# A fourth stage of edges in a four-layer graph network on one core

## The chip, the cores and the metric

The kernel runs on one NeuronCore of one Trainium2 chip. The metric is the device time of one execution, in microseconds (us). The kernel before took 7771.67 us, the median of 10 runs (7760.12 to 7788.72).

## What is computed

A graph has 12,500 nodes with 32 features and 400,000 edges, sorted by their destination. Four layers follow each other; each adds its result to the node features and normalises them. Cut to what matters here:

```python
edge_index = jnp.stack([src, dst])
x = _layernorm(x + _L0_gnn_ref(x, src, dst, ...))       # attention
x = _layernorm(x + _L1_gnn_ref(x, edge_index, 3))       # 3 rounds of means
x = _layernorm(x + _L2_gnn_ref(x, edge_index, edge_attr_32, W1, b1, W2, b2))
x = _layernorm(x + _L3_gnn_ref(x, edge_index))          # 3 rounds of weighted sums

# L2, the edge layer
h = relu(concatenate([x[rol], x[col], edge_attr]) @ W1 + b1)
v = h @ W2 + b2
x_cand = segment_max(v, col)                            # maximum over a node's edges
return maximum(x_cand, x)

# L3, one of its three rounds
x = segment_sum(norm[:, None] * x[src], dst)
```

The destinations are drawn as 12500 u², so low node numbers have many edges and the last ones few.

## The kernel before, in words

**Blocks and counts.** The nodes lie in 98 blocks of 128. A matrix of counts `A` (how many edges lead from node to node) is built in DRAM in layer 0, as 25 chunks of 512 destinations, each with all 98 source blocks. A round of layers 1 and 3 is then a dense product: for each chunk, each of its four quarters of 128 destinations, and each source block, one matmul with the counts as weights and `x3` (the node values as three bfloat16 parts side by side, 96 columns) as moving data (L369). A few pairs that don't fit in `A` go through an extra matrix `Ax`: one row of 392 matmuls ahead of the chunks (L364) and 16 small ones in each chunk (L271). `post3` then scales a chunk and makes the next round's `x3` from it, on VectorE and ScalarE (`split`, L253 to L257).

**The edge layer.** The 308 columns of 128 edges that lead to the first block are handled apart (`heavy`). The other 2817 columns are cut into stages. A stage is a range of edges, laid out as 128 runs side by side, one on each partition. `cuts` (L212 to L217) gives each stage's end: enough columns that all edges to the nodes below block `HS[s]` lie inside it, with five standard deviations to spare. With `HS = (52, 78)` the cuts are 308, 2292, 2804 and 3125: stages of 1984, 512 and 321 columns. Inside `edge_layer`, the plan cuts a stage into batches of up to 48 columns, and a batch into groups of four. For each group POOL gathers four source rows (`ef`, L110, called in `fetch`), TensorE transposes them (L1705), and two matmul layers follow (L1736 to L1760). A batch's destination rows are filled in by 32 scans (`spread`, L1582), its maxima taken by 32 scans (`maxima`, L1591).

**What sets the order.** Python generators are advanced by hand, once for each group: `fill(0)` and `fill(1)` (work of other layers), `steps(6)` (the queue of scans) and `tick()` (ends of stages). When the last maxima of a stage are through, `end(s)` joins the ticked ones. It carries maxima over the borders between the 128 runs: three transposes, a gather `fx`, a maximum, a scatter, spread over 13 ticks, so that nothing has to wait for a transfer. `done(s)` follows: it gathers the maximum at each node's last edge (`ends`, one gather for each node block), and finishes the nodes of blocks `hs[s]` to `hs[s+1]`: norm, scale, `split` into `x3`. Then these blocks can already take part in round 0 of layer 3, and `round_part(s)` joins the fillers: for each of the 25 chunks, `x3` of each block as weights and the counts of that block (128 x 512) as moving data (L1320), then eight small matmuls that add up and turn the result (L283), a copy on ScalarE (L1327) and an addition into `part` on VectorE (L1305). Its counts come in tiles `a` with room for `HP` blocks, three in rotation (L1314, L1315); a chunk's blocks are divided evenly over as few tiles as fit.

```python
            size = -(-(hi - lo) // -(-(hi - lo) // HP))
```

`fill` advances the fillers by 16 matmuls for each group (40 once at the start of a part). After the last group the queues are drained in this order:

```python
    steps(10 ** 6)
    while later:
        tick()
```

and, behind `edge_layer`, `while fillers: fill(0)`. The last stage has no early part. Its blocks are done in round 0 proper:

```python
            R.product(x3, post3, (), 0 if r else HS[-1])
```

Round 0 multiplies only source blocks from `HS[-1]` on (its `lo`), loads only their counts (L351), and `post3` adds `part`. Its row L364 over `Ax` still needs all 98 blocks.

The instructions come into each engine's queue in an order that a scheduler draws up at compile time: program order is the priority, and an instruction whose inputs come late in the scheduler's reckoning lets later ones go ahead. Tiles of a closed pool give their memory to the next one, whose first writer then waits for the last reader.

Of the kernel before, what the change touches and what calls it, by code (L numbers as in the profile page):

```python
# [57 lines left out]

SPAN = 60.0
ONE = 512.0  # L60
HS = (52, 78)
EARLY = 2
HC = 308
SLOTS = 512
# [3 lines left out]
@with_exitstack  # L68
def gnn_resnorm_kernel(
    ctx: ExitStack,  # L70
    tc: tile.TileContext,
    x: bass.AP,
    src: bass.AP,
    dst: bass.AP,
    edge_attr: bass.AP,
    w1T: bass.AP,
    w1_b: bass.AP,
    w2: bass.AP,
    w2T: bass.AP,
    w2_b: bass.AP,  # L80
    aT: bass.AP,
    m_W1: bass.AP,
    m_b1: bass.AP,
    m_W2: bass.AP,
    m_b2: bass.AP,
    out: bass.AP,
):
    nc = tc.nc
    E = src.shape[0]
    flags = ctx.enter_context(tc.tile_pool(name="flags", bufs=1))  # L90
    bad_i = flags.tile([P, 1], I32, name="bad_i")
    dense_path(tc, bad_i, x, src, dst, edge_attr, w1T, w1_b, w2, w2T, w2_b, aT,
               m_W1, m_b1, m_W2, m_b2, out)
    general = nc.values_load(bad_i[0:1, 0:1], min_val=0, max_val=E)
    with tc.If(general > 0):
        general_path(tc, x, src, dst, edge_attr, w1T, w1_b, w2, w2T, w2_b, aT,
                     m_W1, m_b1, m_W2, m_b2, out)
# [22 lines left out]
def dense_path(ctx, tc, bad_i, x, src, dst, edge_attr, w1T, w1_b, w2, w2T, w2_b, aT,  # L120
# [90 lines left out]

    hs = (0,) + HS + (H,)  # L212
    cuts = [HC]
    for h in HS:
        f = (h * P / N) ** 0.5
        cuts.append(-(-int(E * f + 5 * (E * f * (1 - f)) ** 0.5) // P // 4) * 4)
    cuts.append(C)  # L217
    heads = []
    for s in range(len(HS) + 1):
        heads.append((  # L220
# [245 lines left out]
    def edge_tables():  # L466

        with tc.tile_pool(name="e_prep", bufs=2) as prep:
            CP = -(-C // 12)
            d0 = prep.tile([P, 1], F32, name="d0", bufs=1)  # L470
            run = prep.tile([P, 1], F32, name="run", bufs=1)
            for s in range(len(HS) + 1):
                e0, Cs = P * cuts[s], cuts[s + 1] - cuts[s]
# [169 lines left out]
    with ExitStack() as build:  # L643
# [164 lines left out]
        def slots():  # L808
# [31 lines left out]
            yield  # L840
            for s, h in enumerate(HS):
                w = slice(h % 4 * (P // W), h % 4 * (P // W) + 1)
# [310 lines left out]
    with ExitStack() as st:  # L1153
# [3 lines left out]
        with tc.tile_pool(name="seg", bufs=1) as seg, \  # L1157
# [18 lines left out]
            nc.vector.tensor_scalar(tot, tot, -1.0, 0.0, op0=OP.add, op1=OP.max)  # L1176
            for s in range(len(HS) + 1):
                sl = slice(hs[s], hs[s + 1])
# [67 lines left out]
    with ExitStack() as st:  # L1246
# [1 line left out]
        ap = st.enter_context(tc.tile_pool(name="l3_a", bufs=3))  # L1248
        psum = st.enter_context(tc.tile_pool(name="psum", bufs=1, space=PSUM))
        G = 8  # L1250
        HP = 16
        fillers = []
        first = []

# [38 lines left out]
        def round_part(s):  # L1293

            lo, hi = hs[s:s + 2]
            size = -(-(hi - lo) // -(-(hi - lo) // HP))
            late = []
# [11 lines left out]
            for c in range(NQ):  # L1309
                nq = min(4, H - c * 4)  # L1310
                y = psum.tile([P, CH], F32, name="y", bufs=2)
                for h0 in range(lo, hi, size):
                    n = min(size, hi - h0)
                    a = ap.tile([P, 4, HP, Q], F8, name="a")  # L1314
                    nc.sync.dma_start(  # L1315
# [1107 lines left out]
```

## Time and profile before

| | us |
|---|---|
| median of 10 runs | 7771.67 |
| the profiled execution | 7785.55 |
| its span | 7783.8 |
| first and last start of an edge gather `ef` | 2940.3, 6601.1 |
| PE / DVE / ACT / POOL busy, whole span | 6703.9 / 3932.2 / 1633.7 / 3531.5 |
| mean granted clock of TensorE | 0.835 |

How to read it: the span is one execution on the chip; 1.75 us of the profiled execution's time lie around it. PE is TensorE, PEld its weight loads, DVE VectorE, ACT ScalarE, POOL GpSimd, SP the engine that issues most transfers; L1320 is line 1320 of the kernel. In a list of groups, a row has the line, engine, operation, what it writes and reads, and the count, then the busy time, the mean duration of one in ns, and the idle time ahead with what ended it. In an order of time, a row starts with start and duration. PE's matmuls overlap, so a run of n matmuls is the better measure of one than its own duration. The granted clock is a share of TensorE's full clock.

### The profile page before, as it was taken

The numbers are of one execution on the slowest core, as the hardware profiler recorded it, in microseconds if no ns is written. First come the engines' busy times: TensorE is split into PE (matmuls) and PEld (weight loads), VectorE is DVE, ScalarE is ACT, GpSimd is POOL, SyncE is SP. The second block draws the span as 40 slices with busy tenths as digits, with TensorE's granted clock in tenths as the row PEclk, the third lists the DMA queues.
The fourth block names the chain that finished last, engine by engine and source line by source line (L and its number), as shares of the span: only waits on it lengthen the run. The fifth ranks groups of instructions, "written<-read, shape, count | busy, mean of one in ns | idle before, by whom it ended". The sixth has DMA issues, their size and how long they took to land. (4 is left out here: it accounts for less than half of the span.)

```text
span 7783.8 us, 196882 instructions
## 1 busy us (share of the span) xinstructions
PE 6703.9 (86%) x85600; PEld 5342.1 (69%) x85600; DVE 3932.2 (51%) x11040; ACT 1633.7 (21%) x3386; POOL 3531.5 (45%) x3445
## 2 busy tenths in 40 slices
PE   6788999898999997888888888778669979799998
PEld 4678999888999994545555555333336636799998
DVE  6999899795443224555555555433343343411121
ACT  1234787100000002222222222211112212100000
POOL 1013400000555517777777777777777776100000
PEclk7889999999999996777777777555569969999999
DMA  1138444889999992222222222211127726699998
GB/s 50 64 126 324 187 200 196 305 322 338 336 352 352 366 340 84 55 62 55 59 55 63 55 54 59 56 54 54 48 73 242 245 72 203 218 351 361 346 358 300
DMA packets 575179, 1447.57 MB, mean 186 GB/s; under 512 B 108407, under 2 KB 269791, under 8 KB 560863
## 3 DMA queue, kind: packets, MB, share of 16 engines
q1 hardware_dynamic: 433200, 1347.10, 47.3%
q0 software_dynamic: 110240, 66.25, 4.3%
q10 hardware_dynamic: 30864, 21.54, 0.9%
q8 instruction: 673, 11.03, 0.6%
q14 instruction: 202, 1.65, 0.1%
HBM read 1155.33 MB, written 279.27 MB: 184 GB/s over the span
## 5 line engine op out<-in xcount | busy, mean ns | idle before, releaser
L110 POOL DMA_INDIRECT ef<-table,ids x2817 | 2675.7, 950 | 883.0 <-issue 646.4
L369 PE MATMUL y<-x,a 128*128 128x96 bf16 x49980 | 2261.6, 207 | 115.7 <-issue 79.4
L369 PEld LDWEIGHTS <-a 128*128 128x128 fp8e4 x49980 | 2177.8, 98 | 147.5 <-issue 106.4
L1705 PE MATMUL pT<-ident,ef 128*96 128x128 f32 x2817 | 768.4, 355 | 583.2 <-DMA ef<-table,ids 564.8
L1705 PEld LDWEIGHTS pT<-ident,ef 128*96 128x96 f32 x2817 | 397.0, 161 | 1040.1 <-DMA ef<-table,ids 702.1
L1707 DVE COPY eT<-pT 96x512 f32<-96x512 f32 x705 | 476.7, 676 | 1047.8 <-PE pT L1705 1047.5
L983 PE MATMUL pa<-oh,ol 128*128 128x196 bf16 x4928 | 725.9, 271 | 120.0 <-DVE oh L973 77.2
L1754 PEld LDWEIGHTS pv<-mw,hT 128*128 128x128 f32 x3208 | 598.0, 260 | 267.3 <-issue 93.9
L989 ACT ACTIVATE at<-pa 128x784 uint16<-128x784 f32 x816 | 646.9, 824 | 508.2 <-PE pa L983 480.9
L277 DVE TENSOR_REDUCE v<-y 128x128 f32<-128x384 f32 (+2 forms) x152 | 83.3, 548 | 1270.5 <-PE y L271 1270.0
L1754 PE MATMUL pv<-mw,hT 128*128 128x64 f32 x3208 | 679.4, 349 | 21.0 <-ACT hT L1741 13.8
L1741 ACT ACTIVATE hT<-ph,mb 128x256 f32<-128x256 f32 x802 | 379.8, 474 | 1326.6 <-PE ph L1738 1301.9
L1019 PE MATMUL y<-x,at 128*128 128x102 bf16 x9604 | 646.1, 210 | 9.9 <-DVE x L257 5.4
L983 PEld LDWEIGHTS <-ol 128*128 128x128 bf16 x4928 | 552.6, 149 | 132.7 <-issue 75.7
L1736 PE MATMUL ph<-eT,mw 96*64 96x256 f32 x1410 | 628.1, 539 | 12.0 <-DVE eT L1707 10.6
L1738 PE MATMUL ph<-eT,mw 96*64 96x256 f32 x1408 | 630.3, 541 | 0.0
L973 DVE TENSOR_TENSOR oh<-bins_h,pl 128x1568 bf16<-128x1568 bf16 x616 | 594.4, 965 | 0.0
L110 POOL DMA_INDIRECT g<-code_d,ws_i x25 | 219.6, 8785 | 790.8 <-DVE ki L760 527.8
L1019 PEld LDWEIGHTS <-at 128*128 128x128 fp8e4 x9604 | 560.3, 98 | 23.2 <-issue 10.6
L115 POOL DMA_INDIRECT sorted_d<-hrow,pos x308 | 368.7, 1197 | 372.5 <-issue 203.5
L1320 PE MATMUL y<-a,x 128*96 128x512 fp8e4 (+1 forms) x1950 | 493.6, 390 | 1.6 <-DVE x L257 1.5
L968 DVE TENSOR_TENSOR ol<-la,lb 128x1024 bf16<-128x1024 bf16 x616 | 419.4, 683 | 73.2 <-PE pa L983 72.6
(406 smaller groups left out, 7000.4 us busy)
## 6 DMA issues: line engine op xcount, KB each, us to landing
a<-A SPq DMA_DIRECT2D x245, 3136.0 KB
A<-at SPq DMA_DIRECT2D x98, 1568.0 KB
a<-A SPq DMA_DIRECT2D x144, 832.0 KB
ef<-table,ids POOLq DMA_INDIRECT x2817
starts_d<-rows SPq DMA_DIRECT2D x44, 1024.0 KB
attr<-in_edge_attr SPq DMA_DIRECT2D x57, 768.0 KB
begin<-starts_d SPq DMA_DIRECT2D x57, 768.0 KB
scan<-o SPq DMA_DIRECT2D x57, 768.0 KB
```

The source lines that it names most:

```text
L110: return nc.gpsimd.indirect_dma_start(out=o, out_offset=None, in_=tab, in_offset=IndirectOffsetOnAxis(ap=idx, axis=0))
L369: nc.tensor.matmul(y[:, q, :], block(h, q - q0), x3[:, h, :3 * F], start=(q + h == first), stop=False)
L973: nc.vector.tensor_tensor(oh, bins_h[:, None].to_broadcast([P, 4, HJ, 2]), pairs(pl[:, t, 0, half * 64 + w0:half * 64 + w0 + 8])[:, :, Non ...
L983: nc.tensor.matmul(pa[:, 2 * b + i, :HJ], ols[t][:, :, :, 4 * u + 2 * b + i].rearrange("p a b -> p (a b)"), ohs[t][:, 2 * u + b, :, i], st ...
L989: nc.scalar.activation(at[:, qd, :, off:off + 8].rearrange("p h (w j) -> p h w j", w=4), pa[:, :, :HJ].rearrange("p w (h j) -> p h w j", h ...
L1019: nc.tensor.matmul(y[0][:, q, :], at[:, q - 2 * half, h, :], x3[:, h, :3 * F0], start=(q + h == 0), stop=(c < EARLY and last and q == 2 * ...
L1320: nc.tensor.matmul(y[:3 * D, :nq * Q], x3[:, h, :3 * D], a[:, :nq, h - h0, :], start=(h == lo), stop=(h == hi - 1))
L1705: nc.tensor.transpose(pT[:3 * D, j, :], B.ef[:, t + j, :], ident)
L1707: behind = nc.vector.tensor_copy(eT[:, :k], pT[:3 * D, :k])
L1736: nc.tensor.matmul(ph[:HID, :ka], mw1, eT[:, :ka], start=True, stop=True)
L1738: nc.tensor.matmul(ph[HID:2 * HID, :k - 2], mw1, eT[:, 2:k], start=True, stop=True)
L1754: nc.tensor.matmul(pv[:, j].rearrange("p h d -> p (h d)"), hT[:, j, :], mw2, start=True, stop=True)
```

## The change

Two constants change. The edge layer's stages now end behind node blocks 52, 78 and 90, and at the last block, 98; so there are four `end`s and `done`s, three early parts (52, 26 and 12 blocks), and round 0 proper starts at block 90. The tiles of counts for the early parts have room for 13 blocks instead of 16.

```diff
-HS = (52, 78)
+HS = (52, 78, 90)
...
-        HP = 16
+        HP = 13
```

With it `cuts`, `hs` and `heads` get one entry more, and with each entry come four small tiles in `heads`, one more tile `lastd`, gathered ahead of the first edge, and one more pass of the loops over stages in `edge_tables`, `slots` and the computation of `end_i`.

## The prediction

> **What bounds the kernel now.** I read the page first (where the early parts and the gathers stand), then busy time by windows, then PE's, DVE's and POOL's order around the end of the edge layer, then the chain that ended last. On the page two groups matter:
>
> ```profile
> L110 POOL DMA_INDIRECT ef<-table,ids x2817 | 2675.7, 950 | 883.0 <-issue 646.4
> ...
> L1320 PE MATMUL y<-a,x 128*96 128x512 fp8e4 (+1 forms) x1950 | 493.6, 390 | 1.6 <-DVE x L257 1.5
> ```
>
> One gather holds POOL 0.95 us plus 0.30 us of issue, so 1.25 us a column. L1320 is the early part of round 0: 78 node blocks by 25 chunks, 1950 matmuls. Windows of the edge layer's end:
>
> ```profile
> 6300.00:6400.00 100.00, 59.57 (x189) 27.96 (x189) 38.09 (x139) 13.17 (x35) 75.76 (x79) 0.57 0.20 54
> ...
> 6500.00:6600.00 100.00, 100.00 (x593) 63.59 (x592) 36.04 (x143) 20.83 (x49) 67.66 (x73) 1.00 0.67 211
> ```
>
> Columns: length, then busy PE, PEld, DVE, ACT, POOL, granted clock, DMA share, GB/s. Where no early part runs, POOL bounds (79 gathers in 100 us). Where the part of stage 1 runs, PE is busy 100 of 100 us at full clock, and POOL gets only 73 gathers through. So PE bounds the last 150 us of the edge layer already. Then PE's own order:
>
> ```profile
> 6629.82 7.09 PE L1320 MATMUL y<-a,x 128*96 128x512 fp8e4 x32
> ...
> 6642.69 2.25 PE L1320 MATMUL y<-a,x 128*96 128x256 fp8e4 x19
> 6645.45 0.63 PE L283 MATMUL z<-S,ys 96*128 96x32 f32 x4 [0.51 <-ACT ys L1327]
> 6656.38 5.87 PE L364 MATMUL y<-a,x 128*96 128x128 fp8e4 x78 [10.29 <-issue]
> ...
> 6682.35 18.81 PE L364 MATMUL y<-a,x 128*96 128x128 fp8e4 x298 [1.40 <-DVE x L257]
> ```
>
> The part of stage 1 isn't hidden to its end: the last edge gather starts at 6601.1, and the part ends at 6645. Then PE is almost idle until 6682, while 20 `ends` gathers (6646 to 6671) and the norm of the last 20 blocks run. The row L364 follows, and the 20-block product until 6825.
>
> **The change, part by part.** *The plan.* The cuts become 308, 2292, 2804, 3008, 3125. Stages 0 and 1 stay. The old last stage of 321 columns (seven batches, 81 groups of four) becomes 204 (44, 44, 44, 44, 28) and 117 (40, 40, 37), again 51 + 30 = 81 groups, in eight batches. Early part loads stay at 13 blocks in stages 0 and 1, since 52 and 26 divide into 13s with HP at 16 or 13: the smaller buffer costs nothing there.
>
> *When the new part can start.* Each group is one turn of `steps(6)` and of `tick()`. The third stage's last batch has 7 turns, 42 steps, against 64 queued (32 maxima of the batch before, 32 scans of the next): 22 are left. The next ten turns take these 22, 32 more scans and 6 of the 32 last maxima; the other 26 need a further half batch. So the maxima end 16 turns after the stage's last gathers. `end` then takes 14 turns to its first `ends` gather. 16 + 14 = 30 is all the turns that the last stage has. The same count for stage 1 gives 28 turns, and the trace shows 6157.5 (last gather) to 6295.2 (first `ends`), 137.7 us, 27.5 turns of 5.0. So the part of blocks 78 to 89 joins the fillers only in the drain, behind the stage-1 part that already overruns. All of it lies in the open behind 6645. Its blocks are ready in time: 12 gathers behind 6601 take 15 us, the norm some 10.
>
> *What it costs.* 32 matmuls of 512 columns in 7.09 us are 0.216 each; eight adders (L283) push the next by 0.81. A chunk of 12 blocks: 12 x 0.216 + 0.81 = 3.40. 24 chunks and a half one (12 x 0.118 + 0.5) make **83.6 us** of PE.
>
> *The row L364 behind it.* Its load waits for the early part:
>
> ```profile
> SPq L351 <- PE y L1320: 4.4, 1, 4.4
> ```
>
> It is issued at 6645.08, and the first matmul starts 11.3 us later. Today this lies under the wait for the last blocks; that cover goes. Its buffer can start when the early buffer under it is read out; with 25 loads more in a ring of three, that would be about two chunks before the end (3.4 + 1.9 = 5.3). Bounds 0 and 11.3; I take 6.0. The row itself is 392 matmuls:
>
> ```profile
> 6816.48 12.23 DMA a<-Ax
> ...
> 6828.85 24.18 PE y L364 x392
> ```
>
> 24.2 us after a pause of PE (21.9 for the same 392 in round 2, without one). I take 24.2.
>
> *The late product.* For 20 blocks a quarter takes PE 0.85 + 0.17 (L271); for 8 it takes 8 x 0.0425 + 0.17 = 0.51, so 2.04 a chunk instead of 4.08. DVE is next:
>
> ```profile
> 6708.87 0.56 DVE L277 TENSOR_REDUCE v<-y 128x128 f32<-128x384 f32 x1 [3.48 <-PE y L271]
> ...
> 6711.36 0.29 DVE L255 TENSOR_TENSOR rest<-v,x 128x128 f32<-128x128 f32 x1 [0.42 <-ACT x L253]
> 6712.02 0.29 DVE L257 TENSOR_TENSOR x<-rest,x 128x128 bf16<-128x128 f32 x1 [0.36 <-ACT x L256]
> ```
>
> One chunk's chain is 6708.87 to 6712.31, 3.44 us, of which 0.78 are waits for ACT. If the next chunk's operations fill these, the period is 2.66; if not, 3.44. I take 2.85, nearer the lower, because the norms of the last blocks (6668 to 6678) are interleaved in just this way. 24 chunks: 68.4 us (63.8 to 82.6). Ahead of the first reduce: 4.4 (L364's end 6701.0 to yx 6705.4) + 4 x 0.17 = 5.1. Behind the last: 3.4. Loads shrink from 640 to 256 KB. The present ones moved 276 GB/s, so 49 of 256 KB need some 47 us, below DVE's 68.
>
> The Trainium skill, "DMA: Bandwidth & Descriptors", section "Measured (HBM→SBUF, 128 partitions, SWDGE, issued from GpSimd)", speaks against shorter loads: 0.95 us for 64 KB, 6.15 for 1 MB; an estimate between them is 2.0 us for 256 KB, so 98 us for 49 one behind the other, 30 more than my term. The rows decide, since several loads are in flight here (0.87 of 16 engines busy); no run shows 256 KB yet.
>
> *Small parts.* One more `lastd` gather ahead of the edges, 1.25 us where POOL bounds. One more fx gather and scatter in the stretch that PE bounds: nothing, as a group takes 5.45 us there where POOL needs 5.0 (without that slack, 2.5). ACT's and DVE's copies for the new part queue with the norm of the last 8 blocks; DVE stood 3.41 us behind such a gather at 6664.7, so 3.4 once (0 to 7). Twelve `ends` gathers leave the drain (15 us), and the last x is ready near 6670 instead of 6682; nothing, because PE is then in the new part.
>
> *The sum*, from 6645.0 to round 1's first L364. Now 6828.85 - 6645.0 = 183.9, which includes 4.2 of waiting for its Ax load behind the last x (6824.6); that load comes early with the DMA queues emptier. New: 83.6 + 6.0 + 24.2 + 5.1 + 68.4 + 3.4 = 190.7. With 1.25 and 3.4: **+11.5 us**. The profiled execution (7785.55 us, span 7783.8 and 1.75 around it) would become 7797.0. It lay 13.9 above the median of the runs; on the median 7771.67 the forecast is **7783.2**.
>
> **The rivals.**
> *PE's clock falls in the late product (slower).* With 2.04 of every 2.85 us busy (72%), PE may lose its full clock. At half clock a chunk is 4.1 us and PE bounds: 24 x (4.1 - 2.85) = +30, so +41.5, 7813. It decides once the granted clock there is under 2.04 / 2.85 = 0.72. For it: from 6300 to 6400 PE was 60% busy at 0.57. Against it: those are f32 matmuls, and the present product holds 1.00 while 87% busy.
>
> [...]
>
> *The next round's Ax row fills PE's pauses.* Up to 24 x 0.8 = 19 us stand idle in the late product; if round 1's 392 matmuls go there, up to 16 us come back: about -5, 7767. Against it: `a` has three buffers and y three, and the row wants two of the first while chunks still turn them over.
>
> *The part is hidden after all.* Were the early part done by 6645, the last x at 6670 would start 24.2 + 5.1 + 68.4 + 3.4 = 101.1, so 6771 instead of 6829: -58, 7714. Against it: the count of turns, and PE's 100% between 6500 and 6645, where 83.6 more don't fit. So the stage changes the layout and hides nothing.
>
> **How the numbers follow.** Within 0.2% (15.5 us, about what a measurement of this kernel can tell from no change) lies 7756 to 7787. Forecast 0.62: its terms' ends give -5 (wait 0, row 21.9, 2.66 a chunk, no queueing) to +35 (11.3, 24.2, 3.44, 7); two thirds of it fall within 0.2%, a third above. Clock 0.20, slower. Ax row in the pauses 0.14, nearly all within 0.2%. Hidden 0.04, faster. Faster 0.06, same 0.53, slower 0.41. The range takes the forecast's ends, down to part of the Ax case and up to part of the clock's: 7762 to 7808.
>
> **What would show it.** L1320 should count 2250, its last 300 all behind the last edge gather and in a stretch of 80 to 90 us with PE near 100%. L369 should count 48804 (1176 less). L364 should follow within 0 to 11 us. The late product should show DVE's period near 2.85 us and PE's clock. Wrong if L1320's new matmuls lie among the edge gathers, if the late product takes over 90 us, or if the edge layer's last gather moves from 6601 by over 5 us.

## The result, and the profile after

The kernel after took 7824.37 us (median of 8 runs, 7814.41 to 7838.1), the kernel before 7771.01 us in the runs beside it: a ratio of 1.0067, 95% interval 1.0058 to 1.0076, so +53 us (45 to 59). The forecast was +11.5 us and 7783.2, the range 7762 to 7808. The direction was right; the size was not, and the time lies outside the range.

The profiled execution of the kernel after took 7818.75 us, its span 7816.6. That is 32.8 us more than the span before, less than the medians differ. About half of this gap lies ahead of the edge layer: the first edge gather starts at 2929.5 instead of 2940.3. Four later profiles on a chip of this speed have it at 2929.4 (ends_late), 2932.1 (cut_74), 2939.6 (all_three) and 2940.6 (ax_mid). Three of these kernels (all but cut_74) are the kernel after up to there, so those 10.8 us are scatter between executions and not a gain.

The page's two groups of the prediction:

```profile
L110 POOL DMA_INDIRECT ef<-table,ids x2817 | 2672.8, 949 | 879.4 <-issue 660.3
...
L1320 PE MATMUL y<-a,x 128*96 128x512 fp8e4 (+1 forms) x2250 | 569.7, 391 | 1.6 <-DVE x L257 1.3
```

The early parts have 2250 matmuls as counted, 300 more, and L369 has 48804. Windows of the kernel after, the third of them the shorter product of round 0:

```profile
6300.00:6400.00 100.00, 66.62 (x205) 31.78 (x205) 37.14 (x137) 13.03 (x36) 75.86 (x80) 0.57 0.18 51
6500.00:6600.00 100.00, 88.27 (x505) 55.30 (x505) 41.08 (x169) 18.31 (x48) 71.20 (x76) 0.93 0.61 184
6781.00:6857.00 76.00, 57.43 (x1168) 53.49 (x1166) 55.82 (x199) 14.63 (x50) 0.00 (x0) 0.95 0.64 180
```

From 6500 to 6600 PE is no longer busy all the time: 88 of 100 us, while POOL got 76 instructions through instead of 73. What the additional ones are, POOL's order of time says (start, duration, then the idle time ahead and its releaser):

```profile
6547.91 0.98 POOL L115 DMA_INDIRECT scan<-fx,fix  x1 [0.30 <-DVE fx L1638]
...
6552.97 0.95 POOL L110 DMA_INDIRECT ef<-table,ids  x1 [0.30 <-issue]
6554.22 0.94 POOL L110 DMA_INDIRECT ends<-scan,end_i  x1 [0.30 <-issue]
...
6561.71 0.94 POOL L110 DMA_INDIRECT ends<-scan,end_i  x1 [0.30 <-issue]
6562.96 0.94 POOL L110 DMA_INDIRECT ef<-table,ids  x1 [0.30 <-issue]
...
6574.19 1.14 POOL L110 DMA_INDIRECT ef<-table,ids  x1 [0.30 <-DVE ends L1264]
```

The 12 `ends` gathers of blocks 78 to 89 (6554 to 6573) stand among the edge gathers, 1.25 us each, and POOL has hardly more than its issue time between instructions there: POOL now sets the pace. The two edge gathers at 6552.97 and 6574.19 are the 92nd and the 97th of the last 117. The same two in the kernel before:

```profile
6566.13 0.94 POOL L110 DMA_INDIRECT ef<-table,ids  x1 [0.30 <-issue]
...
6573.33 0.94 POOL L110 DMA_INDIRECT ef<-table,ids  x1 [0.37 <-DVE ids L1683]
```

Counted from the first of the 117 (6431.16 after, 6443.76 before), the stream after is 0.56 us ahead at the 92nd gather, although `fx` and its scatter already lie in it, and 13.46 behind at the 97th. At the last it is 13.49 behind. So the whole lengthening of the stream falls where the 12 `ends` gathers stand. Then PE's order around the third part:

```profile
6643.68 2.25 PE L1320 MATMUL y<-a,x 128*96 128x256 fp8e4 x19
...
6665.48 1.88 PE L283 MATMUL z<-S,ys 96*128 96x32 f32 x8 [7.45 <-DVE part L1305]
6667.18 5.18 PE L1320 MATMUL y<-a,x 128*96 128x512 fp8e4 x12
...
6673.00 2.77 PE L1320 MATMUL y<-a,x 128*96 128x512 fp8e4 x12
...
6740.85 0.73 PE L1320 MATMUL y<-a,x 128*96 128x256 fp8e4 x5
...
6752.45 24.42 PE L364 MATMUL y<-a,x 128*96 128x128 fp8e4 x392 [9.73 <-DMA a<-Ax]
...
6863.80 23.41 PE L364 MATMUL y<-a,x 128*96 128x128 fp8e4 x392 [9.46 <-DMA a<-Ax]
```

The first line is the end of stage 1's part, as before near 6646. Behind it lies the whole third part, to 6741.6, with one stall of 7.45 us in which PE waits for VectorE; then 9.73 us of waiting for the `Ax` load, the row L364, the product, and round 1's row at 6863.8 instead of 6828.85. VectorE shows what PE waited for:

```profile
6652.04 0.29 DVE L1305 TENSOR_TENSOR part<-part,z 128x128 f32<-128x128 f32 x1 [4.71 <-PE z L283]
6663.79 0.43 DVE L1263 TENSOR_TENSOR ends<-ends,rest 128x256 f32<-128x256 f32 x1 [11.46 <-DMA ends<-scan,end_i]
...
6665.06 0.28 DVE L1305 TENSOR_TENSOR part<-part,z 128x128 f32<-128x128 f32 x1
```

It stood 11.46 us at the first operation of the last `done` (L1263, blocks 90 to 97) for its `ends` gathers, and the part's addition L1305 was queued behind. And SP's order has the two `Ax` loads, one early and one late:

```profile
6741.71 0.97 SPq L351 DMA_DIRECT2D a<-Ax  x2
...
6851.40 1.38 SPq L351 DMA_DIRECT2D a<-Ax  x2
```

The first is issued only when the last matmuls of the part are through (6741.58), since its tile lies on a tile of the part (ax_apart, below, shows this). The second is issued 2.9 us ahead of the product's last matmuls.

**Where the time is, in the two profiles.** The last 117 edge gathers (the new last stage) take 170.8 us from first to last start instead of 157.3: +13.5. From the last edge gather (6601.1 and 6602.0) to round 1's row L364 it is 261.8 us instead of 227.75: +34.1. Behind that it is -2.2, and between the first edge gather and the 117 columns -1.8. That is 44 us, at the lower end of the interval of the medians.

### The profile page after: what moved, and what is told of

Its sections match the earlier page's. It is cut to its first block, busy times and chain, and to the rows that moved or that the text cites. A ratio compares the mean times of both kernels' runs of the same rounds, so it can differ in the third digit from the quotient of the medians.

```text
span 7816.6 us, 195765 instructions
## 1 busy us (share of the span) xinstructions
PE 6719.1 (86%) x84924; PEld 5329.9 (68%) x84924; DVE 3940.9 (50%) x11152; ACT 1648.2 (21%) x3414; POOL 3518.7 (45%) x3449
## 4 chain that ended last, share of the span: by engine, by line
PE 49%; DMA 14%; POOL 7%; issue 5%; DVE 3%; ACT 0%; DVEq 0%; POOLq 0%; ACTq 0%; SPq 0%
PE y L369 23%; DMA ef<-table,ids 11%; POOL ef L110 6%; PE y L1320 5%; PE pv L1754 5%; PE ph L1736 4%; PE pT L1705 3%; PE ph L1738 2%; PE z L1447 1%; PE y L364 1%; DMA a<-A 1%; PE y L271 1%; PE z L283 1%; PE pT L1419 1%; POOL ends L110 1%
## 5 line engine op out<-in xcount | busy, mean ns | idle before, releaser
L369 PE MATMUL y<-x,a 128*128 128x96 bf16 x48804 | 2204.5, 207 | 119.3 <-issue 76.3
L369 PEld LDWEIGHTS <-a 128*128 128x128 fp8e4 x48804 | 2122.3, 98 | 148.9 <-issue 100.0
L1019 PE MATMUL y<-x,at 128*128 128x102 bf16 x9604 | 644.5, 209 | 10.8 <-DVE x L257 6.1
L1736 PE MATMUL ph<-eT,mw 96*64 96x256 f32 x1410 | 619.4, 532 | 11.1 <-DVE eT L1707 11.1
L1738 PE MATMUL ph<-eT,mw 96*64 96x256 f32 x1408 | 621.6, 534 | 0.0
L1019 PEld LDWEIGHTS <-at 128*128 128x128 fp8e4 x9604 | 559.1, 98 | 24.2 <-issue 11.9
L1320 PE MATMUL y<-a,x 128*96 128x512 fp8e4 (+1 forms) x2250 | 569.7, 391 | 1.6 <-DVE x L257 1.3
```

Source lines behind the costliest of these rows:

```text
L369: nc.tensor.matmul(y[:, q, :], block(h, q - q0), x3[:, h, :3 * F], start=(q + h == first), stop=False)
L1019: nc.tensor.matmul(y[0][:, q, :], at[:, q - 2 * half, h, :], x3[:, h, :3 * F0], start=(q + h == 0), stop=(c < EARLY and last and q == 2 * ...
L1320: nc.tensor.matmul(y[:3 * D, :nq * Q], x3[:, h, :3 * D], a[:, :nq, h - h0, :], start=(h == lo), stop=(h == hi - 1))
L1736: nc.tensor.matmul(ph[:HID, :ka], mw1, eT[:, :ka], start=True, stop=True)
L1738: nc.tensor.matmul(ph[HID:2 * HID, :k - 2], mw1, eT[:, 2:k], start=True, stop=True)
```

## The experiments

The theory: the loss is the third part in the open, with three waits that the prediction had priced too low: VectorE's queue in the part, the `Ax` load, and the 12 gathers in the stream. The rivals: the finer split costs time wherever the part lies; or the smaller tiles do.

The four sets ran on four chips. On three of them the kernel before takes 9061.6 to 9161.5 us, on one 7779.5; every ratio is against runs of the kernel before on the same chip. The last column is from one profile of each kernel and compares only on one chip: where the stream is the same, it still differs by up to some 11 us between the slower profiles. Only where the stages end as in the kernel after are the last 117 gathers a stage of their own.

| run | time, us | ratio to before | 95% interval | last 117 gathers, us |
|---|---|---|---|---|
| kernel before | 7771.01 | 1 | | 157.3 |
| kernel after | 7824.37 | 1.0067 | 1.0058 to 1.0076 | 170.8 |
| hp13 | 9150.62 | 0.9994 | 0.9982 to 1.0005 | 194.3 |
| split_only | 9171.74 | 1.0017 | 1.0005 to 1.0029 | 211.8 |
| fill_drain | 9218.6 | 1.0064 | 1.0040 to 1.0087 | 209.4 |
| ax_apart | 9224.45 | 1.0067 | 1.0045 to 1.0088 | 220.9 |
| after_beside | 9121.38 | 1.0072 | 1.0052 to 1.0092 | 209.1 |
| norm_later | 9118.95 | 1.0068 | 1.0049 to 1.0087 | 220.2 |
| norm_later_apart | 9114.57 | 1.0064 | 1.0046 to 1.0082 | 213.9 |
| cut_70_82 | 9077.29 | 1.0017 | 1.0005 to 1.0029 | 193.8 |
| ends_late | 7827.21 | 1.0060 | 1.0046 to 1.0073 | 171.3 |
| ax_mid | 7816.01 | 1.0051 | 1.0037 to 1.0065 | 170.2 |
| all_three | 7816.49 | 1.0046 | 1.0033 to 1.0060 | 171.9 |
| cut_74 | 7765.98 | 0.9986 | 0.9976 to 0.9996 | 151.5 |
| ends_behind | 9113.66 | 1.0043 | 1.0028 to 1.0058 | 204.9 |
| split_behind | 9067.44 | 1.0001 | 0.9988 to 1.0014 | 195.4 |
| four_edits | 9101.72 | 1.0036 | 1.0024 to 1.0048 | 195.9 |
| cut_76 | 9058.32 | 0.9989 | 0.9976 to 1.0002 | 185.5 |

### One part of the change alone

**hp13**: the kernel before with the smaller tiles.

```diff
-        HP = 16
+        HP = 13
```

> The kernel before with room for 13 blocks in the early parts' tiles instead of 16, and three stages as before. Theory (the loss is the third part in the open, the 12 gathers in the stream and the wait for Ax): no part of it is here, so 7771 within 8 us; L1320 stays at 1950, and round 1's row L364 starts near 6829. Rival (the smaller tiles, by the memory they shift, cost the time): most of +53 us, about 7810 or more.

Measured 0.9994, on a slower chip: no difference. The tiles are out as a cause of the loss.

**split_only**: the kernel after without its third part; the blocks from 78 on are done in round 0 again.

```diff
-            if s < len(HS):
+            if s < 2:
...
-            R.product(x3, post3, (), 0 if r else HS[-1])
+            R.product(x3, post3, (), 0 if r else HS[1])
```

> The kernel after with its four stages, but without the early part of blocks 78 to 89: round 0 starts at block 78 again. Theory: +12 us from the 12 ends gathers among the edge gathers, less some 10 because the last done has 8 blocks and not 20, and +1 for one lastd gather: 7771 to 7779, with L1320 at 1950 and L369 at 49980. Rival (the finer split itself, with its eighth batch, its fourth end and the order that the scheduler makes of it, costs the time, and not where the part lies): 7805 to 7824.

Measured 1.0017 (1.0005 to 1.0029), between the two: by the middle of the interval the split alone costs a quarter of the loss, and the part with its waits the rest. Its last 117 gathers took 211.8 us against 194.3 in hp13 on the same chip, +17.5. Here too the place is clear: the stream is 0.7 us behind hp13's at the 92nd of the 117 and 15.5 at the 97th, with the 12 `ends` gathers between them. So it is these gathers, and not the eighth batch or the fourth `end`, that lengthen it.

**after_beside**: the kernel after, unchanged, on one of the other chips.

> The kernel after, unchanged, on the chip of the other runs of this set, so that each of them has its own comparison. If the chip is like the first, 1.0067 times the kernel before. On a chip that grants the edge layer less clock (0.55 instead of 0.7) the tail behind the last edge gather should cost the same +34 us, since it runs at full clock there too, and the edge gathers' last 117 columns +12 to +23: a ratio of 1.005 to 1.007.

Measured 1.0072: the loss is there too.

### The stall in the part, and the wait for Ax

**fill_drain**: the part is written among the last ticks.

```diff
     while later:
         tick()
+        fill(0)
```

> The kernel after, with a fill(0) behind each tick of the drain, so that the third part is written into the program among the last done's steps and not behind them. Theory: the 7.5 us in which PE stands while VectorE waits for the last ends gather go, and most of the clock lost behind them: -8 to -12 us against the kernel after, about 7814. Rival (the wait only moves, since the norm of the last 8 blocks has then to be waited for later, or the part's additions are still queued behind it): within 3 us of 7824.

A miss: PE still stood 6.68 us for VectorE, which still stood 10.96 us at the last `done`'s first operation with the part's additions behind it. So writing the part elsewhere in the program didn't change that order; how the scheduler came to it isn't shown. The rival holds for this edit.

**ax_apart**: 2 KB a partition ahead of layer 3's tiles.

```diff
         R = Rounds(st, 1)
+        st.enter_context(tc.tile_pool(name="pad", bufs=1)).tile([P, 512], F32, name="pad")
         R.open(st)
```

> The kernel after, with 2 KB a partition left empty ahead of layer 3's tiles, so that Ax's first tile doesn't lie on the third of the early parts' tiles. Theory: the load L351 is issued at least one chunk before the early part's end, the 9.7 us in which PE waits for it shrink to 0 to 3, and the row L364 takes 22 to 24 us: -7 to -11 us against the kernel after, about 7815. Rival (the load waits for something else, or row L364 then waits for x of the last blocks): within 3 us of 7824.

The total didn't fall (1.0067), but not for the rival's reason. PE's order of this run:

```profile
8061.00 6.69 PE L1320 MATMUL y<-a,x 128*96 128x512 fp8e4 x19 [6.13 <-DMA a<-A]
8084.50 1.92 PE L283 MATMUL z<-S,ys 96*128 96x32 f32 x8 [16.81 <-ACT ys L1327]
...
8169.27 10.92 PE L364 MATMUL y<-a,x 128*96 128x128 fp8e4 x192 [0.31 <-DVE part L1305]
```

and VectorE's:

```profile
8076.72 0.43 DVE L1263 TENSOR_TENSOR ends<-ends,rest 128x256 f32<-128x256 f32 x1 [21.28 <-DMA ends<-scan,end_i]
```

The wait for `Ax` is gone (0.31 us). But the part's own first load came 6.13 us late, and this time the order had the last `done` further ahead of its gathers: VectorE stood 21.28 us, ScalarE's copies behind it, and PE 16.81. What one wait gave, two others took.

**norm_later**: the last `done` is ordered on VectorE behind the twelfth addition of the part (`adds` collects the additions of L1305).

```diff
+            if s == len(HS):
+                while fillers:
+                    fill(0)
             for t in todo:
                 yield from finish(*t)
...
+                    with tc.issue_after(adds[-14].ins):
+                        nc.vector.tensor_mul(e, e, over(rest[:, sl], k))
```

> The kernel after, with the finish of the last 8 blocks ordered behind the twelfth addition of the third part (14 from its end), so that VectorE no longer stands at the last ends gather with the part's additions queued behind it. Theory (the stall in the third part is that queueing): the part from its first L1320 to its last takes 83 to 86 us instead of 95, the wait for Ax stays near 9.7: -9 to -12 us against the kernel after. Rival (PE is held by the loads of counts or by ACT's copies in any case): the part stays at 93 or more, within 3 us of the kernel after.

From the end of stage 1's part to the end of the third it is 86.2 us, against 92.9 in after_beside on the same chip and 95.7 in the first profile: the stall was VectorE's queue, and the 83.6 us priced for the part itself were nearly right. Four of these us came back between row L364 and round 1's row (112.1 us instead of 107.9), and the medians (9118.95 and 9121.38) can't tell the two kernels apart.

**norm_later_apart**: both edits.

> The same, and 2 KB a partition left empty ahead of layer 3's tiles, so that Ax's first tile lies apart from the early parts' tiles. In the run with the empty 2 KB alone the wait for Ax went from 9.7 to 0.3 us, but VectorE stood 21.3 us at the last ends gather, and what was won was lost. Theory (two separate waits, the second hidden by nothing once the first is ordered away): -18 to -22 us against the kernel after, about 1.004 times the kernel before. Rival (a wait only moves to the next resource): no more than -10.

A miss: 6.8 us below after_beside in the medians, inside both intervals. SP's order says where it went:

```profile
7925.35 0.37 SPq L351 DMA_DIRECT2D a<-Ax  x1
...
7932.81 1.99 SPq L351 DMA_DIRECT2D a<-Ax  x1
```

The two `Ax` loads (3136 KB each) are now issued ahead of the part's loads, and PE waits for these instead:

```profile
7938.64 5.83 PE L1328 MATMUL y<-a,x 128*96 128x512 fp8e4 x19 [6.56 <-DMA a<-A]
```

The part took 99.4 us. A load of 6.3 MB that starts early is no gain where it stands in front of the loads that are needed first.

**ax_mid**: as norm_later_apart, with the `Ax` loads ordered on SP behind the part's sixteenth load.

```diff
+                    with tc.issue_after(loads[-10].ins) if lo and c < 0 else ExitStack():
                         nc.sync.dma_start(
```

> As the run with the later norm and the empty 2 KB, with the two Ax loads ordered on SP behind the sixteenth of the third part's 25 loads of counts. There they were issued ahead of the part's own loads, whose first then came 6.6 us late. Theory (the 6.3 MB of Ax are hidden only where they neither hold up the part's loads nor come behind them): the part takes 84 to 88 us and the row L364 follows within 3 us: -17 to -20 us against the kernel after, 1.0045 to 1.005 times the kernel before. Rival (DMA is full in the part, and Ax delays the loads wherever it stands): no more than -8.

1.0051 instead of 1.0067, some 12 us and not the 17 to 20 expected. Against ends_late (below), which is the kernel after in effect and ran on the same chip, it is 11 us in the medians, and the intervals overlap:

```profile
6717.94 6.95 PE L1330 MATMUL y<-a,x 128*96 128x512 fp8e4 x19 [3.96 <-DMA a<-A]
...
6752.31 22.09 PE L365 MATMUL y<-a,x 128*96 128x128 fp8e4 x392 [0.31 <-DVE part L1315]
```

The row (here line 365) follows at once and takes 22.09 us. The `Ax` loads still hold up one load of counts in the middle of the part, 3.96 us and the clock behind it, so that the part takes 94.4 us. From the end of stage 1's part to round 1's row it is 203.6 us, against 217.9 in the kernel after.

### The gathers in the stream

**ends_late**: `done` of stage 2 is written behind the last edge gather (`drained` is filled there).

```diff
             todo = []
+            while s == 2 and not drained:
+                yield
```

> The kernel after, with the done of stage 2 (blocks 78 to 89) held back until the last edge gather is written, so that its 12 ends gathers stand in the drain and not among the edge gathers. Theory (each ends gather in the stream pushes every later edge gather by its 1.25 us): the last 117 columns are 10 to 15 us shorter than in the kernel after, the third part still starts behind that of stage 1, and the total falls by the same 10 to 15: 1.005 to 1.0055 times the kernel before instead of 1.0067 to 1.0072. Rival (POOL isn't the bound there, PE is, or the gathers are only moved in front of the third part): no change against the kernel after.

No change beyond the intervals, but it tells nothing about the cost: the trace has the 12 gathers among the edge gathers all the same (6562.9 to 6581.6, the last `ef` behind them). Written later is not issued later: the order in which the program is written didn't decide where they stand.

**all_three**: ax_mid and ends_late.

> The three edits together: ends gathers in the drain, last norm behind the twelfth addition of the third part, Ax load behind its sixteenth load. Theory: -27 to -35 us against the kernel after, so still +20 to +30 against the one before (1.002 to 1.0035): what is left is the third part itself, some 84 us in the open against some 43 us from the shorter product and what the early part's end used to cover. Rival (the three waits cover each other): no better than the best of them alone.

1.0046, a miss: no better than ax_mid within the intervals. The gathers stood in the stream here too.

**ends_behind**: the gathers are tied on POOL behind the last edge gather, besides being written later.

```diff
+                    with tc.issue_after(drained[0].ins) if s == 2 else ExitStack():
+                        gather(nc, e[:, h, :], scan[:P * cuts[s + 1] - HE],
+                               end_i[:, h0 + h:h0 + h + 1])
```

> The kernel after, with the 12 ends gathers of blocks 78 to 89 tied on POOL behind the last edge gather. (Only written later, they were issued among the edge gathers all the same, so that run changed nothing.) Theory (they take POOL's time from the edge gathers where POOL bounds): the last 117 columns take 154 to 160 us as in the kernel before instead of 168, the third part still starts behind that of stage 1, -8 to -12 us against the kernel after: 1.005 to 1.0057 times the kernel before. Rival (the fourth stage slows the stream by its scans, its extra batch or PE's work): the last 117 columns stay at 166 or more and the ratio at 1.0065 or more.

Now they are moved:

```profile
7902.03 0.95 POOL L110 DMA_INDIRECT ef<-table,ids  x1 [2.77 <-DVE part L1310]
7903.29 0.95 POOL L110 DMA_INDIRECT ends<-scan,end_i  x1 [0.30 <-issue]
```

The ratio fell to 1.0043 (1.0028 to 1.0058), more than expected, but on another chip than the 1.0067 and 1.0072 that it is held against. The length that was expected (154 to 160 us) was that of the faster chip. Here the last 117 took 204.9 us, and no run on this chip has the 12 gathers in the stream to compare with.

**split_behind**: ends_behind without the third part (the edit of split_only).

> Four stages without the third early part (round 0 starts at block 78), and the 12 ends gathers of blocks 78 to 89 tied behind the last edge gather, so that the 20 ends gathers stand together as in the kernel before. Theory (what the finer split cost by itself, 1.0017, was these gathers among the edge gathers): 0.9990 to 1.0008 times the kernel before. Rival (the eighth batch, the fourth end, the schedule cost it): 1.0013 or more.

1.0001, and 1.0 lies well inside its interval, while it lay outside that of split_only. With the gathers tied behind, the eighth batch, the fourth `end` and another schedule cost nothing that is measured here. By the ratios alone this would be weak, since the two intervals overlap and the chips differ. The table's last column agrees: on the slower chips the six runs with the 12 gathers of blocks 78 to 89 in the stream took 209.1 to 220.9 us for the last 117, the six without them there 185.5 to 204.9. The firm evidence is the place of the jump, between the 92nd and the 97th gather.

**four_edits**: ax_mid with ends_behind.

> The three edits together (1.0046 times the kernel before, with the ends gathers still in the stream), now with the 12 ends gathers tied behind the last edge gather. Theory: 8 to 12 us less, 1.0030 to 1.0037: what is left is the third part in the open. Rival (the gathers in the drain hold up the third part's start or the last norm): 1.0043 or more.

1.0036, inside what was expected. The 12 gathers are out of the stream, VectorE's stall is gone and the row waits 0.32 us, and the kernel is still slower. But not every wait is gone: the `Ax` loads hold up two loads of counts (4.06 and 0.75 us), so that the part takes 96.9 us, and round 1's row still waits 8.17 us. What the part would cost without any wait was not run. An estimate from the best figures of these runs, from the end of stage 1's part to round 1's row: the part 86.2 (norm_later), the first `Ax` load 1.5 and row and lead 29.4 (ax_mid), the chunks 70.5 + 2.8 and, as before, 4.2 for round 1's `Ax` load, in all 194.6 us against 183.9. So it would still be some 11 us slower, because the part in the open costs more than the shorter product gives back.

### Other cuts

**cut_70_82**: `HS = (52, 70, 82)`.

> The kernel after with its four stages ending behind blocks 52, 70 and 82 instead of 52, 78 and 90: the stage that hides the parts is longer. By the count of turns the part of stage 1 joins the fillers some 60 turns before the last gather and that of stage 2 is done six turns before it. Theory (what counts is whether the early part lies beside the edge gathers): L1320 at 2050 with none behind the last gather's groups, round 0's product has 16 blocks, 3.4 us a chunk: 82 us instead of 76, but 95 + 9.7 us of open part go, and the old 45 us too: -80 to -110 us against the kernel after, -30 to -60 against the one before. Rival (four stages cost by themselves, or PE has no room for it among the gathers): no faster than the kernel before.

1.0017 (1.0005 to 1.0029): some 44 us faster than the kernel after on the same chip, about half of what was expected, and no faster than the one before, as the rival had it. Its tail did shrink, from the last edge gather to the end of the span 1157.1 us against 1212.8 in after_beside. The stream didn't: 4665.1 us from the first to the last edge gather, 4662.2 in after_beside. Whether the additional early blocks cost the stream on this chip, where it is slower anyway, can't be said without a profile of the kernel before there.

**cut_74**: `HS = (52, 74)`, three stages.

> Three stages, ending behind blocks 52 and 74 (and 98). By the count of turns the part of stage 1 is written 22 turns before the last gather, so that none of it is in the open; round 0's product has 24 blocks, 4.8 us a chunk on PE, 114 us instead of 98. Theory: the 45 us that the part of stage 1 stands behind the last gather today overlap the last stage's end, of which little can be saved, so the tail is 0 to 15 us shorter and the total within 0.2% of the kernel before. Rival (the overrun of the early part is all loss): -30 us or more.

0.9986, 0.9976 to 0.9996: within the 0.2% expected, and a little faster than the kernel before. No early part is in the open, yet PE has to wait for the last blocks:

```profile
6647.93 1.09 PE L364 MATMUL y<-a,x 128*96 128x128 fp8e4 x8 [22.90 <-DVE x L257]
...
6659.00 1.09 PE L364 MATMUL y<-a,x 128*96 128x128 fp8e4 x8 [9.43 <-DVE x L257]
...
6662.73 19.08 PE L364 MATMUL y<-a,x 128*96 128x128 fp8e4 x302 [1.92 <-DVE x L257]
```

So the 44 us by which stage 1's part ran over in the kernel before were largely cover for the last stage's end, as the expectation had it: from the last edge gather to round 1's row it is 223.5 us instead of 227.75.

**cut_76**: `HS = (52, 76)`.

> Three stages, ending behind blocks 52 and 76 (and 98). By the count of turns the part of stage 1 (24 blocks) is still written wholly ahead of the last gather, by 12 turns instead of 22, and round 0's product has 22 blocks instead of 24. Theory (hidden early blocks are free, late ones cost 24 x 4 x 0.0425 = 4.1 us each): 8 to 11 us less than with the cut at 74, 0.997 to 0.9975 times the kernel before. Rival (the part then reaches past the last gather again, or PE's work takes POOL's time earlier): no faster than with the cut at 74, 0.9982 to 0.999.

0.9989, 0.9976 to 1.0002, on a slower chip: the rival's figure. Two blocks more in the hidden part gave nothing that shows between different chips. Between cuts at 74 and 78 the time is flat within the intervals; by these neither cut beats the kernel before by more than 0.24%.

## Why the prediction was wrong

*Right:* the counts of matmuls; that the third part joins only in the drain and lies wholly behind the last gather; its own length (83.6 us; 86.2 without the stall); the row L364 after a pause (24.2; 24.4); nothing for the smaller tiles; and that the change hides nothing. The clock rival was nil: 0.95 from 6781 to 6857. So were the rivals that round 1's row fills PE's pauses (it starts 6.6 us behind the last `x`) and that the part is hidden.

*Right by luck:* 2.85 us a chunk of the shorter product, where 2.94 was measured. VectorE sets the pace of the first three chunks only (6783.92 to 6791.72, 2.6 us each). Behind them it waits for PE, and PE for the loads of counts (who waits for whom from 6785 to 6857: us in total, times, longest):

```profile
PE y L369 <- DMA a<-A: 15.9, 23, 1.8
DVE v L277 <- PE y L271: 14.8, 17, 2.8
```

So behind the first chunks the loads, and not VectorE, set the pace. The prediction priced them at 47 us, at the 276 GB/s of the loads of 640 KB. Those of 256 KB came at 180 GB/s while PE stood waiting for them. SP in turn waited 24.5 and 20.2 us for PE to read tiles out before it issued the next, so PE and the loads wait for each other. The last edge gather, whose move by over 5 us was to be a sign of error, stayed near 6601 (6602.0) by luck too: this execution began its gathers 10.8 us earlier, and the stream from first to last gather is 11.7 us longer.

*The step that failed first:* "Twelve `ends` gathers leave the drain (15 us) [...] nothing". They don't vanish where they leave. The prediction's count of turns put them behind the last edge gather ("12 gathers behind 6601"), 30 turns behind their stage's last gathers; the trace has the first of them at 6554.22, 23 groups of four into the last stage. There POOL pays 12 x 1.25 us for them. The prediction took PE for the bound of that stretch, with 0.45 us of slack on POOL a group, and spent that slack on `fx` and its scatter alone. For these two it was enough: the stream is 0.56 us ahead when the `ends` gathers begin. For the 12 it wasn't. POOL's waits for VectorE's `ids` between 6420 and 6620 fell from 16.3 us (19 waits) to 5.0 (6), and the stream is longer by 13.5 us, where the prediction had 1.25 (for `lastd`). hp13 and split_only show the same jump at the same place, and split_behind, without these gathers there, shows no loss.

*The terms that were mis-sized*, in the two profiles, from the end of stage 1's part on:

| term | predicted | measured |
|---|---|---|
| third part, with the queue of the last `done` | 83.6 + 3.4 | 95.65 (6645.93 to 6741.58) |
| wait for the first Ax load | 6.0 | 10.9 |
| row L364 and lead to the first reduce | 24.2 + 5.1 | 31.5 |
| 24 chunks | 68.4 | 70.5 |
| last chunk's end | 3.4 | 2.8 |
| wait for round 1's Ax load | 0 | 6.6 |
| sum | 194.1 | 217.9 |

With `lastd`, 195.35 - 183.9 = +11.5 was the forecast; with the longer stream, 217.9 - 183.9 + 13.5 = +47.5 was measured. The sum with every term at its upper end was only +35: the stream and round 1's `Ax` load were not terms of it, and the part with its stall exceeds even 83.6 + 7. The queue behind the last `done` was named, and priced by the wait of the kernel before (3.41 us). But there PE had nothing to do in it; here it stops the part, because the additions stand behind the same wait on an engine that works in order. The `Ax` wait had its upper bound at 11.3, and the measured value is next to that bound: the estimate supposed that the buffer comes free two chunks early, and the trace has the issue at the last matmul of the part. For round 1's load the prediction said that it comes early "with the DMA queues emptier". It didn't: from its issue to the first matmul of the row it is 12.4 us in both profiles. The load takes the next tiles of a ring of three, so it is issued a number of half chunks before the end, and shorter chunks make that lead shorter: 5.8 us ahead of the last `x` (6851.4 and 6857.2) where it was 8.1 (6816.5 and 6824.6).

The Trainium skill, "TensorE: Matmul & The Clock Gate", section "Why this matters for your kernels", has it that a pause of PE over some 3 us costs the clock. Behind the 7.45 us stall twelve matmuls took 5.18 us instead of 2.77, and the row L364 took 24.42 us after a wait of 9.73 and 22.09 us in ax_mid after 0.31. This agrees, and a stall of that kind costs some 2.3 to 2.4 us more than its length here.

*What stays open.* The two profiles account for 44 us (47.5 in the two stretches named) and the medians give 53 (45 to 59); single profiles scatter by as much as the rest. What the 12 gathers cost as a ratio was measured on other chips than the first. Why they were issued among the edge gathers, ahead of their turn, isn't shown.

## What to carry to other kernels

Work that is moved out of one stretch has to be priced where it goes, on each engine's queue, with that stretch's bound after the move and not before it. A wait that costs nothing today, because its engine had nothing else to do, costs its full length once useful work is queued behind it. And an early part earns only what lies beside other work: behind the last gather it is only traded, here 84 us for 42 us of a shorter product (115.7 us from the first reduce to the last `x` before, 73.3 after), and cover is lost besides. A term that comes out right can still have the wrong bound behind it: who waits for whom says whether it does.

## What the runs showed of the hardware

Chips differ far more than kernels here: 7771 to 7780 us against 9061 to 9162 for the kernel before. The difference lies ahead of round 0, mostly in the edge layer. Much the same stretch of the stream, from some 65 us behind its first gather on, in the kernel after on a chip of each kind:

```profile
3000.00:3500.00 500.00, 414.34 (x2198) 255.61 (x2198) 270.42 (x1076) 128.94 (x337) 378.10 (x401) 0.72 0.22 56
```

```profile
3300.00:3800.00 500.00, 367.75 (x1650) 226.34 (x1650) 200.16 (x783) 96.73 (x254) 283.07 (x301) 0.60 0.17 40
```

The second chip grants TensorE 0.60 instead of 0.72 and gets 301 gathers through instead of 401; the gathers themselves last the same, and POOL waits for VectorE's `ids` instead:

```profile
L110 POOL DMA_INDIRECT ef<-table,ids x2817 | 2667.9, 947 | 1926.7 <-DVE ids L1683 910.2
```

(this row is hp13's). Why the clock is lower there, and whether that belongs to these chips for good, isn't shown. From the last edge gather on, both kinds take nearly the same: 1182.7 us in the kernel before, 1189.8 in hp13.

Loads of 256 KB, of which no run of the kernel before had any in the product, moved 180 GB/s with the DMA engines busy 0.64 of the time, where the loads of 640 KB in the kernel before moved 276 GB/s at 0.88. PE waited for them 23 times, 15.9 us in all, so they held the loop up although the engines weren't full; more than three tiles in rotation were not tried. The estimate of 98 us for 49 of them one behind the other, which the prediction worked out from the Trainium skill, "DMA: Bandwidth & Descriptors", section "Measured (HBM→SBUF, 128 partitions, SWDGE, issued from GpSimd)", was too long, as several are in flight: the whole loop of chunks took 70.5 us. But its direction, that shorter loads are slower than the prediction's 47 us, was right.
